# Two levels' pair products in one burst: a second place for the recurrence's factors, results in their operands' buffers, and a scheduler that knows turns of shape

## The chip, the cores and the metric

The kernel runs on one core of one Trainium2 chip. The metric is the device time of one execution in microseconds, taken as the median of several runs. TensorE (PE) multiplies matrices, and its weight loads have a row of their own (PEld); VectorE (DVE), ScalarE (ACT) and GpSimd (POOL) work on tiles of 128 partitions in on-chip memory; SyncE (SP) issues the DMA transfers. Each engine executes its own queue in order, and waits of one engine for another go over semaphores.

## The reference, cut to what matters

The input is x with 2 batches of 4096 tokens and 256 channels. Two layers of a recurrent block (time mixing, then channel mixing) are followed by a gated feed-forward part whose operands are rounded to blockwise FP4, both parts with an adaptive layer norm around them. The centre of the time mixing is this recurrence, for 4 heads of 64 channels each:

```python
def step(state, inp):
    rt, kt, vt, wt = inp
    kv = kt[..., :, None] * vt[..., None, :]
    out = jnp.einsum('bhk,bhkv->bhv', rt, state + u[None, :, :, None] * kv)
    return (state * wt[..., None] + kv, out)
```

Around it, per layer:

```python
sx = _shift(x) - x
mix = jnp.tanh((x + sx * p['x_maa']) @ p['tm_w1'])   # five small mixing products from it
wx, kx, vx, rx, gx = (x + sx * (p[n] + m) for n, m in ...)
r = sigmoid(rx @ Wr); k = kx @ Wk; v = vx @ Wv; g = silu(gx @ Wg)
w = exp(-exp(time_decay + tanh(wx @ td_w1) @ td_w2))
x = x + (norm(recurrence(r, k, v, w, time_first)) * gn_w + gn_b) * g @ Wo
x = x + sigmoid(xr @ cWr) * (square(relu(xk @ cWk)) @ cWv)   # channel mixing
...
x = x + gb * fp4_linear(silu(fp4_linear(h, w_gate)) * fp4_linear(h, w_up), w_down)
```

## The kernel before, in words

**Tiles.** A tile is 256 tokens (TT) of one batch, two chunks (C) of 128, with the 256 channels in two halves (J) of 128. There are 16 tiles per batch, so 2 layers x 2 batches x 16 tiles = 64 recurrences (`wkv`, line 799), and 32 tiles for the feed-forward part, in half tiles of 128 tokens (`ffn_chunk`, line 1304).

**The recurrence without a loop over tokens.** In a chunk of 128 tokens the product of the decays between a token s and a later token t is split by levels: at level l tokens are paired in groups of 2^l, and `r` and `k` carry the decays up to that level as factors. For each level `products(l)` (line 820) multiplies the `k` of one group with the `r` of the next on PE, with 64 rows of weights (one head) and 32 or 64 columns; a level is 32 matmuls for l = 0 to 4, 16 for l = 5, 8 for l = 6. They go into the PSUM tile `pa`. After each level DVE multiplies the totals of the decays into half of the factors, in place (`pair_view`, line 767, and the `tensor_tensor` into `upd` in line 852), and forms the totals of the next level in `tots`. Masks then pick the valid pairs out of `pa` into `diag` (DVE, `copy_predicated`, line 869), ACT copies them into `attn`, and PE multiplies `attn` with `v`, adds what the state `S` gives, and forms `kv`, the chunk's part of the next state.

Level 0 uses copies of `r` and `k` in which every second token carries the bonus `time_first` (`with_bonus`, line 772, on ACT) in two slots, so it does not need the first update's place: levels 0 and 1 are issued together after the update of l = 0. Each further level is issued by itself, since the update of l overwrites the factors that `products(l)` reads:

```python
for m in {0: (), 1: (0, 1)}.get(l, (l,)):
    products(m)
...
upd = pair_view(rk, h, n)
pl.vector.tensor_tensor(upd, upd, tv..., ALU.mult)
```

A lock (`head_lock`) lets one recurrence at a time be written down, since `pa`, `kv`, `diag` and `attn` exist once.

**The order of the work.** No engine's order is written by hand. Generators (streams) for each layer and batch, for the feed-forward inputs, its chunks, its weights and the conditioning record operations into `Plan` (line 113), which keeps a queue for each stream and gives out one operation at a time (`run`, line 320). It estimates when an operation could start, from costs (`weight`, line 386), dependencies (`need`, line 187, on bounding intervals of the operands) and free engines, and takes among the operations of an engine that could start within `SOON` of the earliest the one of the least lateness, then the oldest. Operations of PE and ACT have a form; a change of form costs `TURN` (PE 94) in its estimate, but does not decide the choice. The estimates set nothing but the order: on the chip semaphores decide.

**Buffers.** Tiles of 128x514 come from a stock of 36 slots, `r` and `k` together from 4 places of their own (`slot2`), the wide feed-forward buffers from 5 (`long`). A stream goes on only while enough slots are free (`LEAST`). Results take a new slot, and the operand's slot is given back after its last reader is written down, for example in `shifted` (line 720: `xn`, then `x`), `time_mix` (line 940: `xx` and `mix`, `xg` and `g`, `xw` and `td`, `xv` and `v`), `channel_mix` (line 1087) and `ffn_chunk` (`hb`, then `hT`).

Of the kernel before, what the change touches and what calls it, by code (L numbers as in the profile page):

```python
# [16 lines left out]
P = 128  # L17
D = 256
J = D // P
TT = 256  # L20
# [14 lines left out]
SLOTS = 36  # L35
STAGGER = (12, 60)
SLOTS2 = 4
TINY = 16
LONG = 5
# [61 lines left out]
class Op:  # L101
    __slots__ = ("eng", "calls", "cost", "port", "wait", "ready", "next", "end", "banks", "tiles", "age", "late", "forms")
# [10 lines left out]
class Plan:  # L113
# [24 lines left out]
    def __init__(self, nc, banks):  # L138
        self.nc, self.banks = nc, [(0.0, b) for b in banks]
        self.probe = banks[0]  # L140
        self.seen = {}
        self.held = {}
        self.free = {e: 0.0 for e in self.ENG}
        self.lock = {"vector": 0.0, "gpsimd": 0.0}
        self.form = {"tensor": None, "scalar": None}
        self.loaded = 0.0
        self.cur = None
        self.count = 0
        for e in self.ENG:
            setattr(self, e, Recorder(self, e))  # L150

    def comes(self, t, when):

        op = Op("load", 0)
        op.next, op.end = None, when
        self.seen[t.name] = [(op, True, 0, P, 0, 1 << 20)]
# [10 lines left out]
    def stock(self, tiles):  # L167
        for t in tiles:
            self.held[t.name] = 0
        return tiles  # L170
# [8 lines left out]
    @staticmethod  # L179
    def region(ap):  # L180
        step, n = ap.ap[0]
        p0 = ap.start_partition()
        lo = ap.offset - p0 * step if n > 1 or step else ap.offset
        hi = lo + 1 + sum((c - 1) * t for t, c in ap.ap[1:])
        return p0, p0 + n, lo, hi

    def need(self, op, ap, writes):
        if isinstance(ap, Later):
            key, probe = ap.bank, ap.probe
            if ap.bank not in op.banks:  # L190
# [7 lines left out]
        p0, p1, lo, hi = self.region(probe)  # L198
        seen = self.seen.setdefault(key, [])
        keep = []  # L200
        for q in seen:
            o, w, a, b, c, d = q
# [3 lines left out]
            if not (writes and hit and p0 <= a and b <= p1 and lo <= c and d <= hi):  # L206
                keep.append(q)
        keep.append((op, writes, p0, p1, lo, hi))
        self.seen[key] = keep
# [8 lines left out]
    def record(self, eng, fn, a, k):  # L218
        st = self.cur
        outs = [k["out"]] if "out" in k else [a[0]]  # L220
        ins = list(a[0 if "out" in k else 1:]) + [v for n, v in k.items() if n != "out"]
        ins = [v for v in ins if isinstance(v, (bass.AP, Later))]
        cost, port = weight(eng, fn, outs[0], ins)
        op = st.last if eng == "tensor" else None
        if op is None or op.next is None:
            self.count += 1
            op = Op(eng, self.count)
            op.late = st.late
            st.queue.append(op)
# [12 lines left out]
        for v in outs:  # L242
            if not is_dram(v):
                self.need(op, v, True)
# [12 lines left out]
    def turn(self, op):  # L257

        return self.TURN[op.eng] if op.forms and op.forms[0] != self.form[op.eng] else 0.0

    def give_out(self, op, t):
# [9 lines left out]
        for fn, a, k in op.calls:  # L271
            fn(*[real(v) for v in a], **{n: real(v) for n, v in k.items()})  # L272
# [35 lines left out]
    def ready(self, streams):  # L308

        can = []  # L310
        for st in streams:
            for op in st.queue:
                if op.wait:
                    continue
                t = self.start(op, st)
                if t is not None:
                    can.append((t, op.late, op.age, op, st))
        return can

    def run(self, streams, stock):  # L320
        streams = [Stream(*q) for q in streams]
        while True:
# [22 lines left out]
            if not can:  # L345
# [8 lines left out]
                (late, age, t, o, st) for t, late, age, o, st in can  # L354
# [3 lines left out]
            self.give_out(op, t)  # L358

# [26 lines left out]
def weight(eng, fn, out, ins):  # L386
# [6 lines left out]
    if eng == "tensor":  # L393
        n, rows, cols = out.free_size(), ins[0].shape[0], out.shape[0]
        if fn == "transpose":
            return 110.0, False
        if rows == P and cols == P:
            return max(4 * n / 2.4 + 6, 195.0 if n == 64 else 265.0 if n == P else 0.0), False
        if n <= 64:
            return {(64, 32): 22.0 if n > 16 else 16.0, (64, 64): 66.0, (P, 64): 70.0}.get((rows, cols), 2 * n), False  # L400
        return 0.55 * (4 * n / 2.4 + 6), False
# [14 lines left out]
    if fn in ("bn_stats", "bn_aggr", "tensor_reduce", "reciprocal"):  # L416
        two = False
    return (205.0 if fn == "scalar_tensor_tensor" and n <= 256 else 150.0) + n / 0.96, two
# [3 lines left out]
def rwkv_adaln_fp4_kernel(ctx: ExitStack, tc: tile.TileContext, a: dict, out: bass.AP):  # L422
# [297 lines left out]
    def shifted(h, ln_w, car):  # L720
# [5 lines left out]
        x_s = take_slot()  # L726
# [5 lines left out]
        give(xn_s)  # L732
# [7 lines left out]
    def lerp(x, sx, maa):  # L740
        m_s = take_slot()
# [25 lines left out]
    def pair_view(rk, h, n):  # L767

        v = rk[:, h : h + 1]
        return bass.AP(v.tensor, v.offset, [v.ap[0], [J * TT - h, 2], [2 * h, n], [1, h]])  # L770
# [28 lines left out]
    def wkv(i, b, rk_s, dec_s, v_s):  # L799
# [3 lines left out]
        r, k = (rk[:, m * J * TT : (m + 1) * J * TT].rearrange(  # L803
            "p (c j t) -> p c j t", c=C, j=J) for m in range(2))
# [4 lines left out]
        r0_s, k0_s = take_slot(), take_slot()  # L809
        r0, k0 = v4(r0_s), v4(k0_s)  # L810
# [8 lines left out]
        at = 0  # L819
        def products(l):  # L820
            R, K = (r0, k0) if l == 0 else (r, k)
# [55 lines left out]
        give(dec_s)  # L877
        tot = tot.rearrange("p (c j) -> p c j", c=C)
# [61 lines left out]
    def time_mix(i, b, h):  # L940
# [9 lines left out]
        give(xx_s)  # L950
        mix_s = take_slot()
# [5 lines left out]
        def to_input(o, maa):  # L957

            m_s = take_slot()
# [8 lines left out]
        def branch_pair(f, g, maa_f, maa_g):  # L968
# [9 lines left out]
            for bk, o, maa in zip(bks, os, (maa_f, maa_g)):  # L978
                ms.append(to_input([o[:, j * TT : (j + 1) * TT] for j in range(J)], maa))
# [14 lines left out]
        give(xg_s)  # L994
        g_s = take_slot()
# [13 lines left out]
        give(xw_s)  # L1009
        td_s = take_slot()  # L1010
# [4 lines left out]
        xk_s, xv_s = branch_pair(1, 2, w["k_maa"], w["v_maa"])  # L1015
# [27 lines left out]
        give(mix_s, x_s, sx_s)  # L1043
# [15 lines left out]
        v_s = take_slot()  # L1059
# [4 lines left out]
        give(xv_s)  # L1064
# [4 lines left out]
        give(o_s)  # L1069
        oT_s = take_slot()  # L1070
# [16 lines left out]
    def channel_mix(i, b, h):  # L1087
# [3 lines left out]
        xr, xr_s = lerp(x, sx, w["cr_maa"])  # L1091
        give(x_s, sx_s)
        yield
        kks = []
        for g in range(FD // P // 2):
# [6 lines left out]
            kks.append(take_slot())  # L1102
# [5 lines left out]
        give(xk_s)  # L1108
        sr_s = take_slot()
# [4 lines left out]
        give(xr_s)  # L1114
# [153 lines left out]
    def ffn_inputs():  # L1268
# [3 lines left out]
        for n in range(B * NT):  # L1272
# [6 lines left out]
            yield from layernorm_rows(x1, xn, rows["cb"][b], lambda c: rows["sb"][b])  # L1279
            p_s = pl.take(long)  # L1280
            yield from fp4(pl, xn_s, C * D, P, scales[0], p_s)
            long.append(p_s)
            xq_s = take_slot()
# [4 lines left out]
            give(xn_s)  # L1288
# [15 lines left out]
    def ffn_chunk(c, b, t, x1_s, xq_s, left):  # L1304
        HF = FI // 2
        cs_ = slice(c * P, (c + 1) * P)
        x1, xqT = v3(x1_s), v3(xq_s)
        hb_s = pl.take(long)
        hb = hb_s[:, :FI]
        for s in range(2):  # L1310
# [13 lines left out]
            yield  # L1324
        p_s = pl.take(long)
        yield from fp4(pl, hb_s, FI, P, scales[1 + c], p_s)
        long.append(p_s)
        hT_s = pl.take(long)
# [11 lines left out]
        long.append(hb_s)  # L1340
# [17 lines left out]


    streams = [(counted(first_layer(b), b, 0), LATE[0], LEAST[0]) for b in range(B)]  # L1360
    streams += [(counted(second_layer(b), b, 1), LATE[1], LEAST[1]) for b in range(B)]
    with tc.manual_schedule():
        for t, src, _ in coming:
            nc.sync.dma_start(out=t, in_=src)
        streams += [(ffn_inputs(), LATE[2], LEAST[2]), *((ffn_chunks(c), LATE[2], 1) for c in range(C)), (ffn_weights(), 2.0, 0), (conditioning(), -1.0, 0)]
        pl.run(streams, stock)
# [48 lines left out]
```

## Time and profile before

| what | value |
|---|---|
| time, median of 3 runs | 3134.46 us (3129.04 to 3141.4) |
| the profiled execution: time, span of its instructions | 3128.25 us, 3126.4 us |
| mean granted clock of TensorE | 0.983 |
| busy time of PE, PEld, DVE | 2995.5, 2400.8, 2386.0 us |
| busy time of ACT, POOL | 1627.4, 947.8 us |
| DMA | 42.51 MB, mean 14 GB/s |
| activation table loads on ACT | 131 of 1283 ns |

In the profile an instruction that `Plan` recorded carries the line of `give_out` (L272), so operations are told apart by their tiles: `pa<-slot` are the pair products of levels 1 to 6, `pa<-slot,slot` those of level 0, `bank<-...` all matmuls into the five rotating PSUM banks. A form 64\*32 means 64 rows and 32 columns of TensorE's array in use. A matmul in the code is two records in the trace, a transpose one. The ends of matmuls are modelled, so that distances between starts tell more than lengths.

### The profile page before, as it was taken

Reading aid. Unit: us, or ns where it says so; the run is one execution under the profiler, and the core shown is the slowest. Engines: PE = TensorE matmul, PEld = TensorE weight load, DVE = VectorE, ACT = ScalarE, POOL = GpSimd, SP = SyncE. Lnnn points to the kernel's source line nnn. Section 1 sums busy time; section 2 is a strip of 40 time slices with the busy share of each in tenths; the row PEclk is TensorE's granted clock in tenths of the full one; section 3 lists DMA queues with packets and bytes.
Section 4 is the critical chain, followed back from the end, with each engine's and each line's share of the span. In section 5 each row is a group of like instructions: output and inputs, shape, how many; then the busy total and the mean of one; then the engine's idle time right before and its main releaser. Section 6 shows DMA issues by size and latency. Waiting matters only on the chain.

```text
span 3126.4 us, 89289 instructions
## 1 busy us (share of the span) xinstructions
PE 2995.5 (96%) x38460; PEld 2400.8 (77%) x38460; DVE 2386.0 (76%) x6146; ACT 1627.4 (52%) x3366; POOL 947.8 (30%) x888
## 2 busy tenths in 40 slices
PE   6899999999999999999999999999999999999977
PEld 4777787787877777777778878778888787787765
DVE  6786777877778777778787777777877877786766
ACT  3555555555555455554555555545555555554432
POOL 2233333232332331333323333332323333332210
PEclk8899999999999999999999999999999999999988
DMA  4000000000000000000000000000000000000000
GB/s 141 23 9 5 14 9 10 9 13 9 10 8 10 13 8 7 16 7 15 5 8 15 7 15 8 14 5 14 7 9 15 8 12 7 9 7 12 10 7 12
DMA packets 35723, 42.51 MB, mean 14 GB/s; under 512 B 2817, under 2 KB 33537, under 8 KB 35329
## 3 DMA queue, kind: packets, MB, share of 16 engines
q1 hardware_dynamic: 35328, 36.81, 3.8%
q8 instruction: 302, 4.95, 0.7%
q14 instruction: 93, 0.75, 0.1%
HBM read 28.41 MB, written 8.39 MB: 12 GB/s over the span
## 4 chain that ended last, share of the span: by engine, by line
PE 81%; DVE 10%; ACT 6%; issue 2%; POOL 1%; DMA 0%; POOLq 0%; DVEq 0%; ACTq 0%; SPq 0%
PE bank L272 72%; PE pa L272 7%; DVE slot L272 5%; ACT slot L272 3%; DVE long L272 2%; ACT attn L272 2%; PE kv L272 1%; DVE tiny L272 1%; DVE scales L272 1%; POOL slot L272 1%; DVE diag L272 1%; ACT L272 0%; POOL tiny L272 0%; ACT long L272 0%; DVE S L272 0%
## 5 line engine op out<-in xcount | busy, mean ns | idle before, releaser
L272 POOL TENSOR_TENSOR slot<-slot,slot 128x512 f32<-128x512 f32 (+1 forms) x448 | 514.6, 1162 | 898.2 <-DVE slot L272 666.2
L272 ACT ACTIVATE slot<-bank 128x512 f32<-128x512 f32 (+2 forms) x644 | 333.0, 521 | 690.2 <-PE bank L272 662.7
L272 POOL TENSOR_TENSOR tiny<-tiny,nhalf 128x2 f32<-128x2 f32 (+1 forms) x288 | 291.5, 1015 | 962.7 <-DVE tiny L272 893.9
L272 DVE TENSOR_TENSOR slot<-slot,slot 128x512 f32<-128x512 f32 x512 | 386.8, 757 | 104.4 <-PE pa L272 86.3
L272 PE MATMUL bank<-slot,small 32*128 32x256 f32 (+3 forms) x2816 | 401.9, 362 | 3.6 <-DVE slot L272 3.1
L272 PE MATMUL bank<-slot,cWk 128*128 128x256 f32 x1536 | 373.1, 389 | 6.9 <-DVE slot L272 6.4
L272 PE MATMUL bank<-cWv,slot 128*128 128x256 f32 x1536 | 343.9, 380 | 0.0
L272 PEld LDWEIGHTS bank<-slot,small 32*128 32x128 f32 (+3 forms) x2816 | 269.6, 178 | 90.6 <-issue 38.9
L272 PEld LDWEIGHTS pa<-slot 64*32 64x32 f32 x19456 | 221.8, 107 | 139.1 <-issue 51.5
L272 PEld LDWEIGHTS bank<-slot,cWk 128*128 128x128 f32 x1536 | 285.5, 193 | 51.4 <-DVE slot L272 7.9
L272 PEld LDWEIGHTS bank<-cWv,slot 128*128 128x128 f32 x1536 | 289.2, 190 | 40.3 <-ACT slot L272 0.3
L272 ACT ACTIVATE slot<-bank,small 128x256 f32<-128x256 f32 (+1 forms) x640 | 251.9, 451 | 79.9 <-PE bank L272 78.1
L272 DVE SCALAR_TENSOR_TENSOR slot<-bank,small,slot 128x256 f32<-128x256 f32 x640 | 274.9, 474 | 23.7 <-PE bank L272 22.7
L272 PE MATMUL pa<-slot 64*32 64x16 f32 x19456 | 263.7, 190 | 30.2 <-DVE slot L272 16.6
L272 DVE TENSOR_TENSOR slot<-slot,bank 128x512 f32<-128x512 f32 x192 | 131.0, 683 | 180.9 <-PE bank L272 159.9
L272 POOL TENSOR_TENSOR slot<-slot 128x512 f32<-128x512 f32 x128 | 141.5, 1106 | 311.6 <-ACT slot L272 217.1
L272 ACT ACTIVATE slot<-slot 128x512 f32<-128x512 f32 x288 | 182.0, 635 | 34.3 <-DVE slot L272 30.0
L272 ACT ACTIVATE slot<-slot,tiny 128x256 f32<-128x256 f32 x256 | 142.0, 594 | 106.3 <-DVE tiny L272 85.5
L272 DVE TENSOR_TENSOR long<-long,bank 128x352 f32<-128x352 f32 x256 | 131.7, 516 | 85.9 <-ACT long L272 64.8
L272 DVE SCALAR_TENSOR_TENSOR slot<-slot,small,slot 128x256 f32<-128x256 f32 x384 | 181.0, 507 | 17.5 <-POOL slot L272 17.4
L272 PE MATMUL bank<-ident,slot 128*128 128x128 f32 x1152 | 177.8, 282 | 12.9 <-ACT slot L272 7.7
L272 PE MATMUL bank<-wd,long 128*128 128x256 f32 x768 | 187.3, 395 | 2.0 <-ACT long L272 1.4
(106 smaller groups left out, 5347.9 us busy)
## 6 DMA issues: line engine op xcount, KB each, us to landing
slot<-in_L_attn_x_dram SPq DMA_DIRECT2D x64, 256.0 KB, 2.8
out_dram<-slot SPq DMA_DIRECT2D x64, 128.0 KB, 1.7
slot<-in_L_wmod_dram SPq DMA_DIRECT2D x6, 256.0 KB, 7.6
cWk<-in_L_attn_cWk_dram SPq DMA_DIRECT2D x2, 768.0 KB, 7.9
cWv<-in_L_attn_cWv_dram SPq DMA_DIRECT2D x2, 768.0 KB, 9.9
small<-in_small_dram SPq DMA_DIRECT2D x2, 718.0 KB, 8.5
long<-in_L_ffn_w_down_dram SPq DMA_DIRECT2D x2, 352.0 KB, 3.1
long<-in_L_ffn_w_gate_dram SPq DMA_DIRECT2D x5, 128.0 KB, 8.1
```

Of the source, the lines that this page charges most:

```text
L272: fn(*[real(v) for v in a], **{n: real(v) for n, v in k.items()})
```

## The change

It has three parts.

1. **A second place for the factors.** One tile `rk2` of 128x1024 takes the factors of levels 0, 3 and 4; the others stay in the `slot2` place (`place`). The update from level 2 to 3 reads one place and writes the other, and so does that from 4 to 5; the half that the update does not multiply is copied by ACT. Products of levels 0 and 1, 2 and 3, and 4 and 5 are recorded together, level 6 by itself. The copies of level 0 go into `rk2` in place of two slots.
2. **Results in their operands' buffers.** `x` takes the slot of `xn`, `mix` of `xx`, `g` of `xg`, `td` of `xw`, `v` of `xv`, `oT` of `o`, the last mixed input that of `sx`, and in the feed-forward part `xq` that of `xn` and `hT` that of `hb`. Slots go from 36 to 37, places for `r` and `k` from 4 to 3, `long` from 5 to 4. Streams wait for a free place or `long` buffer before they take one.
3. **The scheduler.** An operation of PE that changes the form is put behind others by `TURNS`, and a turn back to 128\*128 costs `BACK` more. Regions of operands are exact bit sets in place of bounding intervals (`spread`). Some costs are set anew. The order of equal lateness gets a random part (`JITTER`), eight orders are drawn up without writing them down (`dry`), and the one whose estimated end is earliest is written.

The core of the diff:

```diff
-SLOTS = 36
+BACK = 104.0
+TURNS = 30.0
+SLOTS = 37
 STAGGER = (12, 60)
-SLOTS2 = 4
+PLANS, JITTER = 8, 8.0
+SLOTS2 = 3
 TINY = 16
-LONG = 5
+LONG = 4
...
-        hi = lo + 1 + sum((c - 1) * t for t, c in ap.ap[1:])
-        return p0, p0 + n, lo, hi
+        dims = tuple((t, c) for t, c in ap.ap[1:] if t and c > 1)
+        return p0, p0 + n, spread(dims) << lo
...
-            hit = a < p1 and p0 < b and c < hi and lo < d
+            hit = a < p1 and p0 < b and c & at
...
+            op.rank = op.age + self.random.uniform(0.0, JITTER)
...
-        return self.TURN[op.eng] if op.forms and op.forms[0] != self.form[op.eng] else 0.0
+        if not op.forms or op.forms[0] == self.form[op.eng]:
+            return 0.0
+        return self.TURN[op.eng] + (BACK if op.forms[0] == (P, P) else 0.0)
...
-                (late, age, t, o, st) for t, late, age, o, st in can
+                (late, age + TURNS * (o.eng == "tensor" and self.turn(o) > 0), t, o, st) for t, late, age, o, st in can
                 if o.eng == op.eng and t <= now + SOON
...
+    rk2 = keep.tile([P, 2 * J * TT], F32, name="rk2")
...
+    def parts(rk):
+
+        return (
+            rk[:, m * J * TT : (m + 1) * J * TT].rearrange("p (c j t) -> p c j t", c=C, j=J) for m in range(2)
+        )
+
+    def pair_view(rk, h, n, changed=True):
+
+        v = rk[:, h : h + 1] if changed else rk[:, :1]
+        return bass.AP(
+            v.tensor, v.offset, [v.ap[0], [J * TT - h if changed else J * TT + h, 2], [2 * h, n], [1, h]]
+        )
...
-        r0_s, k0_s = take_slot(), take_slot()
-        r0, k0 = v4(r0_s), v4(k0_s)
+        r0, k0 = parts(rk2)
+        r, k = parts(rk)
...
+        place = {0: rk2, 1: rk, 2: rk, 3: rk2, 4: rk2, 5: rk, 6: rk, 7: rk}
+
         def products(l):
-            R, K = (r0, k0) if l == 0 else (r, k)
+            R, K = parts(place[l])
...
-            for m in {0: (), 1: (0, 1)}.get(l, (l,)):
+            for m in {1: (0, 1), 3: (2, 3), 5: (4, 5), 6: (6,)}.get(l, ()):
                 products(m)
-            if l == 1:
-                give(r0_s, k0_s)
...
-            upd = pair_view(rk, h, n)
+            here, there = place[l] if l else rk, place[l + 1]
+            if here is not there:
+                pl.scalar.copy(pair_view(there, h, n, False), pair_view(here, h, n, False))
             pl.vector.tensor_tensor(
-                upd, upd, tv.rearrange("p n m -> p m n").unsqueeze(3).to_broadcast([P, 2, n, h]), ALU.mult
+                pair_view(there, h, n), pair_view(here, h, n), tv.rearrange("p n m -> p m n").unsqueeze(3).to_broadcast([P, 2, n, h]), ALU.mult
             )
...
-        x_s = take_slot()
+        x_s = xn_s
...
-        v_s = take_slot()
+        v_s = xv_s
...
-        hT_s = pl.take(long)
+        hT_s = hb_s
...
+    def plan(seed, dry):
+
+        pl.begin(seed, dry)
...
+        return max(pl.free.values())
+
+    best = min(range(PLANS), key=lambda seed: plan(seed, True))
```

More of the change, by code (lines that the diff above doesn't have):

```diff
@@ L101 @@
 class Op:
-    __slots__ = ("eng", "calls", "cost", "port", "wait", "ready", "next", "end", "banks", "tiles", "age", "late", "forms")
+    __slots__ = ("eng", "calls", "cost", "port", "wait", "ready", "next", "end", "banks", "tiles", "age", "late", "forms", "rank")
     def __init__(self, eng, age):
@@ L358, in run, with spread @@
             self.give_out(op, t)
+@lru_cache(None)
+def spread(dims):
+    m = 1
+    for t, c in reversed(dims):
+        k, out = 1, m
+        while k < c:
+            s = min(k, c - k)
+            out |= out << t * s
+            k += s
+        m = out
+    return m
 class Stream:
@@ L1307, in ffn_chunk @@
         x1, xqT = v3(x1_s), v3(xq_s)
+        while not long:
+            yield
         hb_s = pl.take(long)
@@ L1324, in ffn_chunk @@
             yield
+        while not long:
+            yield
         p_s = pl.take(long)
@@ L1364, in rwkv_adaln_fp4_kernel @@
             nc.sync.dma_start(out=t, in_=src)
-        streams += [(ffn_inputs(), LATE[2], LEAST[2]), *((ffn_chunks(c), LATE[2], 1) for c in range(C)), (ffn_weights(), 2.0, 0), (conditioning(), -1.0, 0)]
-        pl.run(streams, stock)
+        plan(best, False)
 def layout(inputs):
```

116 lines of the change are left out of this document (67 added, 49 removed).

## The prediction

> **What bounds the kernel now.** I read the page's engine row and slices first, then the windows by stage, then PE's timeline.
>
> ```profile
> span 3126.4 us, 89289 instructions
> PE 2995.5 (96%) x38460; PEld 2400.8 (77%) x38460; DVE 2386.0 (76%) x6146; ACT 1627.4 (52%) x3366; POOL 947.8 (30%) x888
> ...
> PE   6899999999999999999999999999999999999977
> ...
> PE 81%; DVE 10%; ACT 6%; issue 2%; POOL 1%; DMA 0%; POOLq 0%; DVEq 0%; ACTq 0%; SPq 0%
> PE bank L272 72%; PE pa L272 7%; DVE slot L272 5%; ACT slot L272 3%; DVE long L272 2%; ACT attn L272 2%; PE kv L272 1%; DVE tiny L272 1%; DVE scales L272 1%; POOL slot L272 1%; DVE diag L272 1%; ACT L272 0%; POOL tiny L272 0%; ACT long L272 0%; DVE S L272 0%
> ```
>
> PE is full in all slices but the first two and the last two, and 81% of the chain that ended last is PE. The windows by stage (time, then busy time and count of PE, weight loads, DVE, ACT, POOL, then PE's granted clock) say how full:
>
> ```profile
> 100.00:200.00 100.00, 91.93 (x1041) 75.21 (x1041) 82.26 (x226) 55.28 (x120) 36.35 (x31) 0.95 0.06 16
> 200.00:2900.00 2700.00, 2651.23 (x34921) 2135.49 (x34920) 2075.49 (x5364) 1459.74 (x3014) 852.22 (x780) 1.00 0.04 10
> 2900.00:3127.00 227.00, 182.49 (x1510) 141.48 (x1508) 158.79 (x351) 77.26 (x153) 35.89 (x35) 0.90 0.03 10
> ```
>
> Between 200 and 2900 us PE lacks 49 us of 2700 and runs at the full clock. So a microsecond taken from PE's own stream is a microsecond of the end, as long as nobody is late for PE. But a busy PE is not a working PE: the ends of matmuls are modelled, so dead time between two shapes of matmul hides in it. The timeline shows it (start, length to the last end, operation, count of records; each matmul in the code is two records):
>
> ```profile
> 1502.35 0.73 PE L272 MATMUL pa<-slot 64*32 64x16 f32 x64
> 1503.01 1.99 PE L272 MATMUL bank<-slot,small 128*128 128x256 f32 x8
> 1504.94 0.45 PE L272 MATMUL pa<-slot 64*32 64x32 f32 x32
> 1505.32 0.66 PE L272 MATMUL bank<-ident,slot 128*128 128x128 f32 x4
> ```
>
> Read starts alone. A record 128x256 in a run of its like takes 0.216 us (16 of cWk from 1530.60 to 1534.06). Eight take 1.73, but from 1503.01 to 1504.94 it is 1.93: the turn from the full shape 128\*128 to 64\*32 costs 0.20. A product record takes 0.0083 (64 of them in 0.53 us when another product level follows, 1491.59 to 1492.12). 64 take 0.53, but 1502.35 to 1503.01 is 0.66: turning back costs 0.13. Over all 268 and 251 such turns of the timeline the medians are **0.198 and 0.129 us**, with the middle half within 0.001; 0.182 is that of leaving 32\*128. A visit of PE to the pair products costs 0.327 us beside its work.
>
> **The change, part by part.**
>
> *Turns of shape.* The instruction order of the two programs can be counted, since the scheduler writes it out. Matmuls are 20016 in both. Runs of one shape: 128\*128 from 597 to 431, 64\*32 from 313 to 189, 32\*128 from 164 to 142, the others from 253 to 241. Separate visits to the tile pa fall from 373 to 252, because levels 0 and 1, 2 and 3, 4 and 5 now stand in one visit. With the price of leaving each shape: 166 x 0.198 = 32.9, 124 x 0.129 = 16.0, 22 x 0.182 = 4.0, the others 1.1: **54.0 us** less. The joined levels alone are 124 x 0.327 = 40.5 of it; the other 13.5 is the scheduler's new dislike of turns (BACK, TURNS), mostly in the small mixing matmuls. All of it lies on PE, which sets the end.
>
> The Trainium skill, TensorEngine Tiling (Array Packing), Key Properties, says that changing the tiling mode drains the array; it gives no price there. TensorE: Matmul & The Clock Gate, Step-by-step, puts the drain at some 128 cycles, which at 2.4 GHz is 0.053 us: an estimate by that page is 0.107 for both turns, and the 54 would be some 18. The row has three times that, and is what I use.
>
> *The waits at the products.* I laid the durations above over PE's order, which gives the PE work from each level's products to the next level's. Against the starts in the trace the median difference is 0.02 us or less for each step, so what is left are waits: 7.4, 12.3, 12.7, 5.2 and 8.0 us over 64 recurrences for the five steps from level 1 to 6, 45.6 together. Steps 2 to 3 and 4 to 5 go (17.5 us). Two of the three steps left now need two updates in a row on DVE, and there the cover counts. Median PE work between the visits is 2.92 us (levels 1 to 2), 2.76 (3 to 4) and 2.06 (5 to 6); before it was 2.05 at most steps.
>
> *The copies.* Levels 3 and 5 need their factors in another place than levels 2 and 4, so the half that is not multiplied is copied by ACT: 2 x 64 = 128 copies of 128x512. The page's rows for the parts:
>
> ```profile
> L272 DVE TENSOR_TENSOR slot<-slot,slot 128x512 f32<-128x512 f32 x512 | 386.8, 757 | 104.4 <-PE pa L272 86.3
> ...
> L272 ACT ACTIVATE slot<-slot 128x512 f32<-128x512 f32 x288 | 182.0, 635 | 34.3 <-DVE slot L272 30.0
> ```
>
> 128 x 0.635 = 81 us on ACT, 52% to 55%: hidden there. What is not hidden: at l=2 the waits written into the program make the update into rk2 wait for the copy into rk2 in 46 of 64 recurrences, and the copy wait for the update in most of the rest; though they touch different halves, they run one after the other. (At l=4 both wait for the same update and run beside each other.) So from the last product of level 1 to the first of level 2 it takes update 0.757, copy 0.635, update 0.757 and four handovers of about 0.1 to 0.15: 2.7 us against the cover of 2.92; 29 of 64 have less than 2.7, and their shortfalls add up to 22 us. Behind the waiting update on DVE stand the next tile's statistics and mixing, for which PE waits too; between the two updates only 0.42 us of other DVE work remains. Ends: 0, if PE's other work covers it, and 64 x 0.83 (copy and two handovers) = 53, if all of it reaches PE. I take 20, near the sum of shortfalls. With the 17.5 saved, waits come out even within 5.
>
> *Buffers.* Results written over operands (x over xn, g over xg, v over xv, hT over hb and so on) add no instruction; each result already had to wait for the readers of that operand. Slots 36 to 37 with fewer taken, long 5 to 4 with hT inside hb, rk places 4 to 3: I cost these at 0. The work of the other streams hides a late buffer; without it, a stream that waits for a third rk place stalls by up to one recurrence. One rk2 for all: the next bonus must wait for the previous level 4; in the trace it starts earlier than that in 9 of 63 cases, by 5.0 us at most, and the bonus stands a median of 12.8 us ahead of its first product. So 0; the other end is 9 x 5 = 45 us of PE idle, far off since four streams feed PE.
>
> *The scheduler.* Exact regions in place of bounding ones, corrected costs, eight orders tried: no cost on the chip. The gain lies between 0 and the 49 us that PE lacks from 200 to 2900. I take 0, since the two other rows of waits are already counted.
>
> *The end.* From 2980 on DVE's fp4 chains set the pace (PE idle 11.5 us before one transpose of long). After the last kv product 9 half tiles of the FFN follow before, 7 after, with 98 and 84 us of PE work, so the tail shrinks with the rest and the 54 is not lost there.
>
> Sum against the profiled execution: it took 3128.25 (span 3126.4 and 1.9 around it). 3128 - 54 - 17 + 20 = 3077. The median shown, 3134.5, lies 6 above that execution; I put the forecast half-way up, at **3080 us**.
>
> **The rivals.**
>
> *The waits eat the gain* (chance 0.15). For it: 57 of 64 gaps between the two updates hold under 0.85 us of DVE work, so DVE stops there. All of the 53 us reach PE and only the 17.5 come back: 3128 - 54 - 17 + 53 = 3110, or 3128 if the gain of the joined steps fails too. Against it: four streams, and waits at the same places cost 0.08 to 0.20 us a step now.
>
> *Slower* (0.05). One mechanism: the stretch from level 1 to level 2. The updates take 1.76 (at 1492.95) and 1.10 (at 1496.39) when POOL works beside them, and an activation table load of 1.283 (131 in the trace) can stand ahead of the copy on ACT. If that were the rule, the stretch needs 1.10 + 1.28 + 0.64 + 1.10 + 0.5 = 4.6 against 2.92: 1.7 x 64 = 109, and 3128 - 54 + 109 = 3183. It decides from a mean of 0.84 us per recurrence (54 / 64). Against it: the mean of the update is 0.757, and there are two table loads per recurrence in some 49 us.
>
> *PE is not the bound* (in the first rival's 0.15). Weight loads are busy 77% of the span and DVE 76%; if PE's turns were slack that waits elsewhere would fill, the time would stay at 3128. Against it: the 49 us of PE idle in 2700, and turns of the same length in every place, which a wait would not have. By the Trainium skill, Perfetto Trace Analysis, Identifying the Most-Contended Engine, matmul busy time is no measure of the distance to the peak and weight loads are the better one, which speaks for this rival.
>
> *More than forecast* (0.20). Half of the 49 us goes as well: 3128 - 54 - 25 = 3049, 3055 as a median.
>
> The change not doing what it says is excluded for the order: the joined visits stand in it, 122 of 64 matmuls and 3 of 128.
>
> **How the numbers follow.** Forecast 0.60 at 3080, its own range 3065 to 3098. The range that should hold 8 in 10 takes in the better case and the first rival's lower part: 3048 to 3118. Half a per cent, about what a measurement can tell here, is 16 us: 3119. Faster: 0.60 + 0.20 + 0.07 of the first rival = 0.87; same 0.08; slower 0.05.
>
> **What would show it.** In the profile after: about 125 fewer rows of pa in the timeline and turns still at 0.198 and 0.129; PE busy near 2940; ACT with 128 copies near 0.64 us; DVE idle before the rk2 update released by ACT. Wrong it would be if PE's idle from 200 to the tail rose from 49 to over 80, or if the update's mean rose above 0.8.

## The result, and the profile after

| what | before | after |
|---|---|---|
| time, median of 20 runs each | 3133.3 us (3129.0 to 3141.4) | 3142.2 us (3131.6 to 3152.1) |
| ratio to before, 95% interval | | 1.0023 [1.0015, 1.0031] |
| span of the profiled execution, mean granted clock | 3126.4 us, 0.983 | 3135.3 us, 0.976 |

The changed kernel is 9 us slower, within the half per cent that counts as no change, where 3080 had been forecast; the range ended at 3118. The traces come from single executions, of 3128.3 us before and 3137.2 after, both about 5 below their medians. The page of the changed kernel, its first rows and slices:

```profile
span 3135.3 us, 89669 instructions
...
PE 2965.8 (95%) x38460; PEld 2417.5 (77%) x38460; DVE 2359.7 (75%) x6146; ACT 1684.7 (54%) x3492; POOL 946.2 (30%) x888
...
PE   6899999999999999999999999999999999998997
```

PE is busy 30 us less and the span is 9 us longer. Its windows (time, then busy time and count of PE, weight loads, DVE, ACT, POOL, then PE's granted clock):

```profile
100.00:200.00 100.00, 90.99 (x952) 75.06 (x952) 72.91 (x213) 52.88 (x111) 32.55 (x31) 0.87 0.05 15
200.00:2900.00 2700.00, 2604.10 (x34592) 2135.37 (x34590) 2040.11 (x5320) 1498.05 (x3103) 838.57 (x767) 0.98 0.03 10
2900.00:3136.00 236.00, 205.34 (x1934) 161.40 (x1934) 179.00 (x416) 97.11 (x196) 51.30 (x49) 0.97 0.04 12
```

Between 200 and 2900 us PE now lacks 96 us, not 49, and gets through 34592 records, not 34921. The clock column fell from 1.00 to 0.98: in the record of the granted clock the time at 0.5 in this stretch rose from 17 to 85 us. PE's waits there (who waits, for whom; us, times, longest), before, then after:

```profile
PE pa L272 <- DVE slot L272: 8.7, 14, 1.5
...
PE pa L272 <- DVE diag L272: 3.7, 3, 2.2
```

```profile
PE pa L294 <- DVE diag L294: 19.3, 21, 2.6
PE bank L294 <- ACT slot L294: 15.4, 20, 2.3
PE pa L294 <- DVE slot L294: 10.2, 10, 3.3
```

The largest is new: products wait until a predicated copy into `diag` is done. One such place in the timeline of the changed kernel (start, length, engine, operation, count, and in brackets the idle time before it with its releaser):

```profile
1599.32 0.71 PE L294 MATMUL pa<-slot 64*32 64x16 f32 x62
...
1599.96 1.56 PE L294 MATMUL bank<-slot,small 32*128 32x256 f32 x12
...
1600.92 0.68 DVE L294 TENSOR_TENSOR slot<-slot,slot 128x512 f32<-128x512 f32 x1
...
1601.52 0.43 DVE L294 COPY_PREDICATED diag<-masks,pa 128x256 f32<-128x256 int32 x1
1601.69 0.62 ACT L294 COPY rk<-slot 128x512 f32<-128x512 f32 x1 [4.82 <-DVE slot L294]
...
1602.34 0.69 DVE L294 TENSOR_TENSOR rk<-slot,slot 128x512 f32<-128x512 f32 x1 [0.39 <-ACT rk L294]
1602.95 0.43 DVE L294 COPY_PREDICATED diag<-masks,pa 128x128 f32<-128x128 int32 x1
...
1603.44 0.76 PE L294 MATMUL pa<-slot 64*32 64x16 f32 x60 [1.92 <-DVE diag L294]
```

Levels 0 and 1 end at 1600.03. Level 1's update runs at 1600.92, then ACT's copy, and level 2's update only when the copy is done (1601.69 + 0.62 = 1602.31; it starts at 1602.34): three steps in a row. The predicated copies of levels 0 and 1 stand on DVE between them, and the products of level 2 wait for the second one, to 1603.38. PE had one piece of other work, and then 1.92 us of nothing. What follows the wait shows in four windows around it:

```profile
1596.60:1600.00 3.40, 3.40 (x142) 2.83 (x140) 2.61 (x7) 0.27 (x1) 1.57 (x1) 1.00 0.00 0
1600.00:1603.40 3.40, 1.52 (x14) 1.04 (x12) 2.70 (x6) 1.69 (x2) 0.97 (x2) 1.00 0.13 43
1603.50:1606.90 3.40, 3.40 (x132) 2.61 (x133) 3.31 (x10) 0.11 (x1) 2.27 (x2) 0.50 0.02 5
1606.90:1610.30 3.40, 3.40 (x46) 2.38 (x45) 2.53 (x5) 1.57 (x3) 1.73 (x2) 1.00 0.00 0
```

PE worked 1.52 of 3.40 us, and in the next 3.4 us its clock is 0.50. PE's rows there:

```profile
1604.05 0.81 PE L294 MATMUL pa<-rk 64*32 64x16 f32 x62
1604.79 2.48 PE L294 MATMUL bank<-wg,slot 128*128 128x352 f32 x4
1607.11 1.89 PE L294 MATMUL bank<-slot,Wg 128*128 128x256 f32 x8
1608.84 1.35 PE L294 MATMUL bank<-wu,slot 128*128 128x352 f32 x4
1610.11 0.73 PE L294 MATMUL pa<-rk 64*32 64x16 f32 x64
```

By the starts, the four records of 128x352 from 1604.79 take 2.32 us, and the four from 1608.84, at the full clock, 1.27. The products are hardly slower: the 128 records from 1603.44 take 1.35 us, where the medians before (2 x 0.53 and a turn back) give 1.2. So the wait cost 1.9 us, and the clock after it some 1.2 more.

**Where the 9 us come from.** As in the prediction I price PE's instructions and turns at their medians before, in program order, and subtract this from the measured distance between the first products of two levels; the rest is waits and lost clock ("excess"), summed over 64 recurrences. The priced order falls from 2939 to 2886 us, so 53 are saved. Excess of the six steps between levels, 0 to 1 first, goes from 5.5, 7.4, 12.3, 12.7, 5.2, 8.0 to 3.9, **46.3**, 1.0, **34.3**, 1.8, **20.8**: 57 us more. From level 6 over kv to the next recurrence it is 25 more, at the start 4 more, behind the last kv 24 less. -53 + 57 + 25 + 4 - 24 = +9.

### The profile page after: what moved, and what is told of

Same layout as the page of the kernel before. It is cut to its first block, busy times and chain, and to the rows that moved or that the text cites. A ratio compares the mean times of both kernels' runs of the same rounds, so it can differ in the third digit from the quotient of the medians.

```text
span 3135.3 us, 89669 instructions
## 1 busy us (share of the span) xinstructions
PE 2965.8 (95%) x38460; PEld 2417.5 (77%) x38460; DVE 2359.7 (75%) x6146; ACT 1684.7 (54%) x3492; POOL 946.2 (30%) x888
## 5 line engine op out<-in xcount | busy, mean ns | idle before, releaser
L294 PE MATMUL bank<-slot,small 32*128 32x256 f32 (+3 forms) x2816 | 391.8, 363 | 13.0 <-DVE slot L294 7.1
L294 DVE TENSOR_TENSOR slot<-slot,slot 128x512 f32<-128x512 f32 x320 | 235.5, 738 | 69.9 <-PE pa L294 37.3
L294 PE MATMUL pa<-slot 64*32 64x16 f32 x11264 | 173.9, 195 | 37.2 <-DVE slot L294 15.8
L294 PEld LDWEIGHTS pa<-slot 64*32 64x32 f32 x11264 | 145.5, 111 | 79.6 <-DVE diag L294 23.7
```

## The experiments

Theory 1: the joined levels themselves make the waits (two updates and a copy in a row, four predicated copies ahead of level 4). Theory 2: the scheduler's edits make them. Theory 3: the buffers. Theory 4: the order drawn is a matter of luck. An edit of the scheduler or of the work changes the whole order, so each run but e3, whose order is that of the changed kernel, has a plan of its own. In the table "priced" is the sum over PE's order as above, "idle" is PE's from 200 to 2900 us, "at 2" is the part of it that lies just ahead of level 2's products, and "half" is the time at granted clock 0.5 in the same stretch; all in us. The last four columns come from one execution each, which lies up to 10 us from the run's median (e12_unpaired 10 below it, e1_place and e13_pa_only 8 above), and "half" differs between executions of one kernel: small differences in these columns tell nothing.

| run | time | ratio to before, 95% | priced | idle | at 2 | half |
|---|---|---|---|---|---|---|
| before | 3133 to 3138 | 1 | 2939 | 49 | 7.1 | 17 |
| after | 3142.2 | 1.0023 [1.0015, 1.0031] | 2886 | 96 | 18.4 | 85 |
| e1_place | 3120.0 | 0.9950 [0.9934, 0.9965] | 2905 | 67 | 1.6 | 96 |
| e2_sched | 3162.5 | 1.0089 [1.0065, 1.0112] | 2926 | 94 | 20.5 | 62 |
| e3_cols | 3143.1 | 1.0023 [1.0009, 1.0037] | 2886 | 97 | 18.2 | 82 |
| e4_nocopy | 3099.6 | 0.9890 [0.9868, 0.9912] | 2882 | 78 | 5.6 | 67 |
| e5_bounds | 3115.0 | 0.9938 [0.9922, 0.9955] | 2884 | 67 | 0.4 | 55 |
| e6_buffers | 3155.3 | 1.0064 [1.0042, 1.0087] | 2906 | 77 | 0.4 | 65 |
| e7_no_turns | 3177.5 | 1.0144 [1.0126, 1.0161] | 2898 | 109 | 26.0 | 86 |
| e8_seed3 | 3155.5 | 1.0075 [1.0060, 1.0090] | 2888 | 95 | 26.0 | 85 |
| e9_more_bufs | 3105.8 | 0.9912 [0.9896, 0.9928] | 2887 | 67 | 0.6 | 55 |
| e10_long4 | 3102.5 | 0.9900 [0.9876, 0.9925] | 2882 | 70 | 0.6 | 48 |
| e11_bufs_alone | 3151.8 | 1.0074 [1.0048, 1.0099] | 2906 | 84 | 0.0 | 68 |
| e12_unpaired | 3138.5 | 1.0012 [0.9999, 1.0026] | 2921 | 64 | 8.8 | 38 |
| e13_pa_only | 3139.8 | 1.0010 [0.9998, 1.0022] | 2880 | 93 | 2.5 | 85 |
| e14_rk_only | 3100.5 | 0.9886 [0.9869, 0.9902] | 2888 | 69 | 3.1 | 51 |
| e15_sched_bounds | 3153.8 | 1.0054 [1.0034, 1.0073] | 2923 | 72 | 7.5 | 58 |
| e16_old_costs | 3135.9 | 0.9989 [0.9977, 1.0000] | 2898 | 77 | 1.8 | 72 |
| e17_one_edge | 3124.9 | 0.9969 [0.9955, 0.9982] | 2882 | 72 | 4.7 | 72 |
| e18_rk_more_bufs | 3071.4 | 0.9794 [0.9780, 0.9809] | 2890 | 57 | 4.1 | 31 |

### One part alone, and the suspects on their own

**e1_place.** Before, with `rk2`, `place`, the joined bursts and the copies, and `-SLOTS = 36` / `+SLOTS = 34`.

> The kernel before with only the second place and the joined levels (old scheduler, old buffers otherwise, 34 slots so that it fits). Theory 1 (the joined levels themselves lengthen the chain between two visits to pa: two updates in a row, the copy ahead of the one at level 2, four predicated copies ahead of level 4; TensorE waits there and its clock is halved afterwards): TensorE's idle from 200 to 2900 us 80 to 110 us and half-clock time there 60 to 100 us as in the changed kernel, time 3120 to 3160. Theory 2 (the scheduler's edits make the waits): idle 40 to 60, half-clock about 20, time 3070 to 3095, which is the time before less the 40 us of turns of shape.

17 us faster than the kernel before beside it (3136.5). Of the 34 us saved in priced order about half arrives. The step 1 to 2 has 23 us of excess, not 46, and PE hardly stands ahead of level 2 (1.6). The half-clock time of 96 us belongs to the slowest of its ten executions (3127.8 us, mean clock 0.972); the median of the mean clock is 0.978 here, 0.979 in the kernel before beside it and 0.974 in the changed kernel, so a usual execution loses hardly more clock than the kernel before. So the joined levels do cost waits, as theory 1 has it, but they gain on the whole.

**e2_sched.** Before, with the third part of the change alone.

> The kernel before with only the scheduler's edits (exact regions, price of a turn, jitter and eight plans, corrected costs), levels and buffers as before. Theory 1: idle and half-clock time as before (about 50 and 20 us from 200 to 2900), time 3105 to 3135, the lower end if fewer turns of shape are made. Theory 2: idle 80 or more, half-clock 60 or more, time over 3150. The scheduler's own estimate of the end is 50 us above that for the kernel before, so by its own reckoning this one is slower: if the chip follows, about 3180.

26 us slower, though its order is priced 13 lower: theory 2 holds for a large part. That -17 and +26 make +9, the whole change, can be chance: results in their operands' buffers are in neither, and each number holds to within the size of a draw of the plan (see e8). Its waits look like those of the changed kernel, without the new joins (levels 2 with 3 and 4 with 5) and without a copy:

```profile
PE pa L294 <- DVE diag L294: 23.9, 28, 2.3
PE bank L294 <- ACT slot L294: 14.1, 22, 2.5
```

**e3_cols.** After, so that levels 0 to 5 share no column of `pa`.

```diff
-        at = sum(wide[0 if l < 4 else 4 : l])
+        at = sum(wide[0 if l < 6 else 6 : l])
```

> The changed kernel, with columns of pa of their own for levels 0 to 5, so that level 4's products no longer wait until the four predicated copies of levels 0 to 3 have read pa. Theory 1: the step from level 3 to level 4 loses about 1.4 us less on VectorE per recurrence, its excess of 34 us falls to about 15, some half-clock time goes with it: 3105 to 3125. If the two updates and not the predicated copies bind there: excess stays near 30, time 3135 to 3145.

No change (excess of 3 to 4: 37, `PE pa <- DVE diag` 23.3 over the whole span against 24.2). My reason was wrong: products and predicated copies that share no element are put in order all the same, so columns of their own do not part them.

**e4_nocopy.** After, without

```diff
-            if here is not there:
-                pl.scalar.copy(pair_view(there, h, n, False), pair_view(here, h, n, False))
```

> The changed kernel with both ScalarE copies between the two places left out, so the half of the factors that an update doesn't change is stale after levels 2 and 4 (the output isn't the reference's). Theory 1: from the end of level 1 to the update of level 2 1.2 us less, the excess of the step 1 to 2 falls from 46 to about 15 us: time 3080 to 3110. Rival (the copies are covered, the two updates bind alone): excess over 35, time 3130 to 3145. Rival (order of the plan): the plan drawn is another one, so a change of more than 25 us at unchanged excess per step would be the order's.

This version leaves half of the factors stale after levels 2 and 4, so it is a measurement and no alternative. 43 us faster than the changed kernel; excess of 1 to 2 is 16. The copies, 2 x 64 of 0.618 us on an engine that is busy 54%, matter, it seems, through the order that they force, since the engine that runs them has idle time left.

### Which of the scheduler's edits

**e5_bounds.** After, with the intervals of the kernel before:

```diff
-        dims = tuple((t, c) for t, c in ap.ap[1:] if t and c > 1)
-        return p0, p0 + n, spread(dims) << lo
+        n1 = 1 + sum((c - 1) * t for t, c in ap.ap[1:])
+        return p0, p0 + n, ((1 << n1) - 1) << lo
```

> The changed kernel, but its scheduler takes the region of an access as the whole interval from its first to its last element again, so it plans the copy and the update at level 2 one after the other, as the chip runs them. Theory 2a (exact regions make the scheduler blind to an order that the program has all the same): the excess of the step 1 to 2 falls from 46 to about 20 us as in the run with the second place alone, half-clock time falls with it: 3110 to 3125. Theory 1 (the joined levels alone): 3135 to 3150.

27 us faster than the changed kernel, excess of 1 to 2 is 20, and PE's waits of pa for `diag` are down to

```profile
PE pa L294 <- DVE diag L294: 3.9, 7, 1.1
```

**e6_buffers.** e5 with `-TURNS = 30.0` / `+TURNS = 0.0` and `JITTER` 0.001.

> The changed kernel with interval regions, no price of a turn and no jitter (one plan): what is left of the change is the second place, the buffers that results take over, and the corrected costs. Next to the run with the second place alone (3120): if the buffers cost nothing, 3110 to 3130. If single slots and fewer buffers bind (theory 3), 3140 or more.

**e7_no_turns.** After, with `-TURNS = 30.0` / `+TURNS = 0.0`.

> The changed kernel with the price of a turn out of the choice of the next instruction (exact regions, jitter and seed as before). It makes some 11 us more of turns by my count. If holding the products back to save a turn is what makes the waits, their sum falls by more than 25 us: 3115 to 3130. If exact regions make them, the excess of the step 1 to 2 stays at 35 or more and the time is 3140 to 3160.

**e8_seed3.** After, with `-    best = min(range(PLANS), ...)` / `+    best = 3`.

> The changed kernel with the plan of another draw (seed 3; its estimated end is 10.4 us above that of the plan taken). If the scheduler's estimate tells plans apart, 3145 to 3160; if draws differ on the chip by their waits and not by the estimate, anything within 30 us of 3142, and this is the size below which two plans tell nothing of a cause (theory 4).

The price of a turn is worth 35 us with exact regions (e7 against after) and, with the draw of plans, 40 with intervals (e6 against e5), though it saves only 12 and 22 us of priced order; it is not what makes the waits. Another draw is 13 us slower: differences of that size between two plans prove no cause. It is a single pair, so the spread of draws may well be wider; and the kernel before, measured beside each group of runs, moved from 3133 to 3138, which adds some 4 us of doubt between groups. In e7 and e8 PE idles 26 us ahead of level 2, in e5 and e6 0.4: that number goes with the regions, whatever the draw.

### Buffers and joining, with interval regions

**e9_more_bufs** is e5 with 34 slots, 4 places, 5 long buffers; **e10_long4** with 35, 4, 4; **e11_bufs_alone** is e6 with the numbers of e9.

> The changed kernel with interval regions (3115 with the buffers of the change) and the second place's bytes taken from 3 of the 37 slots instead: 34 slots, 4 places of the recurrence's factors, 5 long buffers. Best of eight plans by the scheduler's estimate (seed 2). If the fewer buffers bind (theory 3), the waits from the products of level 6 to the next recurrence's level 0 (36 and 56 us of excess) shrink by some 20 us: 3085 to 3105. If not, within 15 us of 3115.

> As the one before with 35 slots, 4 places of the factors and 4 long buffers as in the change (seed 1, the scheduler's estimate 4 us lower). If the places of the factors bind, as the one before; if the long buffers do, 10 us or more over it.

> The run with interval regions, no price of a turn and no jitter (3155), with 34 slots, 4 places of the factors and 5 long buffers. The one difference is the numbers of buffers. Theory 3: back to 3120 to 3130, as with the second place alone. If results that take their operands' buffers, or the corrected costs, lose the time: 3145 or more.

9 and 13 us faster than e5, but e11 only 3 faster than e6 (by the ratios to the kernel before, 3 slower): all within the size of a draw. Theory 3 is not confirmed; these runs can't tell whether the numbers of buffers are worth anything. e6 and e11 stay 32 to 35 us above e1, which the next group takes up.

**e12_unpaired.** e5 with levels 2 to 5 a burst each:

```diff
-        place = {0: rk2, 1: rk, 2: rk, 3: rk2, 4: rk2, 5: rk, 6: rk, 7: rk}
+        place = {0: rk2, 1: rk, 2: rk, 3: rk, 4: rk, 5: rk, 6: rk, 7: rk}
...
-            for m in {1: (0, 1), 3: (2, 3), 5: (4, 5), 6: (6,)}.get(l, ()):
+            for m in {0: (), 1: (0, 1)}.get(l, (l,)):
```

> The changed kernel with interval regions (3115), but levels 2 to 5 each a burst of their own as in the kernel before, and no copy between the places (the second place holds level 0's factors alone). If joining is worth its turns less the waits that I saw (34 less some 17): 3130 to 3145. If joining cost more than it saved (theory 1 in full): under 3110.

23 us slower than e5. Joining is worth about that: 37 us of priced order, less what its waits cost. It is more than a draw, and e1 points the same way without the new scheduler, so theory 1 in full, that joining costs more than it saves, has fallen.

### Which order the exact regions lose

In the built programs one can read what each instruction waits for. In the changed kernel the first products of level 2 wait for a predicated copy in 52 of 64 recurrences; under intervals (e5) always for level 1's update. At l=2 the update waits for the copy in 47 and the copy for the update in 17; e5 has the copy first in all 64, since its plan knows that the two do not run together. The traces agree: 47 and 64 copies start ahead of their update, and in neither kernel do the two overlap once.

**e13_pa_only**, **e14_rk_only.** After, with intervals for one kind of tile:

```diff
+        if ap.name.startswith("pa"):                # e14: (("rk2", "slot2"))
+            n1 = 1 + sum((c - 1) * t for t, c in ap.ap[1:])
+            return p0, p0 + n, ((1 << n1) - 1) << lo
```

> The changed kernel with interval regions for pa alone (exact ones elsewhere, the best of eight plans by the scheduler's estimate, seed 3). In the built program of the changed kernel the first products of level 2 wait for the predicated copy of level 1 in 52 of 64 recurrences, because the planner, with exact regions, puts the predicated copies of levels 0 and 1 ahead of them; here they wait for level 1's update in all. If that order is the larger part of the 27 us of exact regions: excess of the step 1 to 2 about 30 us, 3115 to 3128. If the copy that the planner takes to run beside its update is: 40 us or more, 3132 to 3145.

> The other half: interval regions for the two places of the factors alone (seed 5), so the planner knows that level 2's update waits for the copy, and the predicated copies still go ahead of level 2's products (56 of 64 recurrences). If the copy's wait is the larger part: 3115 to 3128; if the predicated copies are: 3132 to 3145.

With `pa` alone nothing is gained (3139.8): the predicated copies stand behind the products again and the idle time ahead of level 2 is 2.5, but the step 3 to 4 has 46 us of excess and idle and half-clock time are as long as before the edit. With the factors alone 42 us are gained, more than with intervals everywhere (27), though the difference is the size of a draw. DVE's update into `rk2` in the changed kernel, then in e14 (count, busy us, mean ns, idle before it and its releaser), and e14's wait for `diag`:

```profile
L294 DVE TENSOR_TENSOR rk<-slot,slot 128x512 f32<-128x512 f32 x64 | 44.2, 691 | 16.6 <-ACT rk L294 16.6
```

```profile
L297 DVE TENSOR_TENSOR rk<-slot,slot 128x512 f32<-128x512 f32 x64 | 44.9, 702 | 3.3 <-ACT rk L297 3.3
```

```profile
PE pa L297 <- DVE diag L297: 4.8, 8, 1.1
```

The update hardly waits for the copy any more, since the plan puts other work between them; the predicated copies still go ahead of level 2's products in e14, and PE hardly waits for them. So in the changed kernel it is an order among the factors that hurts, most likely the copy's, and the wait for `diag` was the last link of a chain that had become late through it. That the copy alone does it is not shown: e14 gives the plan all orders of the factors, and e2, which has no copy, waits as long for `diag` (23.9 us).

**e15_sched_bounds**: e2 with e5's diff. **e16_old_costs**: e11 with the costs and the price of a turn of before.

> The kernel before with the scheduler's edits but interval regions (the run with exact ones took 3162; the scheduler's estimates of the two differ by 0.3 us). No joined levels and no copies here. If exact regions let predicated copies go ahead of products also in this kernel: excess of the steps 1 to 2 and 2 to 3 from 32 and 23 back to some 10 each, time 3120 to 3140. If not: 3155 or more.

> The run with 34 slots, no price of a turn, no jitter and interval regions (3152), with the instruction costs and the price of a turn that the scheduler of the kernel before had. What it has of the change beyond the second place (3120) is then only that results take their operands' buffers. If the corrected costs lost the 32 us: 3110 to 3130. If the shared buffers did: 3145 or more.

e15 is 9 us faster than e2, and its excess of the steps 1 to 2 and 2 to 3 is 16 and 18 (32 and 23 in e2). The waits at these steps go with exact regions here too, but 9 us of time is less than a draw, and 17 us of the scheduler's loss stay. e16 is 16 us faster than e11, and by the ratios to the kernel before beside each, 1.0074 and 0.9989, it is 27. So the corrected costs may take half of those 32 us or more; the rest, between e16 and e1, may be shared buffers or the draw. Neither is more than hinted at by one plan each.

**e17_one_edge.** After, and the plan is told one thing:

```diff
+                copied = pl.cur.queue[-1]            # after pl.scalar.copy(...)
...
+            if l == 2:
+                pl.edge(copied, pl.cur.queue[-1])    # after the update
```

> The changed kernel with one edge added to the planner's graph: level 2's update comes after level 2's copy (exact regions stay, everywhere; best of eight plans by the estimate, seed 1). If this one order that the program keeps and the plan did not know is what the interval regions of the factors gave back (3100): 3100 to 3115, excess of the step 1 to 2 from 46 to about 25 us. If it was another order among the factors: 3125 to 3145.

17 us faster than the changed kernel, 10 short of what I expected; excess of 1 to 2 is 39.5, not 25. PE's idle time fell from 96 to 72, that ahead of level 2 from 18.4 to 4.7, and DVE's update waits 1.6 us for the copy, not 16.6. The one edge takes the waits at its place away. It does not give all of e14's gain, and part of the waiting only moves: within the step 1 to 2, over the whole span, PE's idle time ahead of level 2 falls from 25 to 5 us, but that ahead of the other work between the two levels rises from 12 to 18, and PE's busy time at half clock there from 15 to 33.

**e18_rk_more_bufs.** e14's diff with 34 slots, 4 places, 5 long buffers (seed 2).

> Interval regions for the two places of the factors alone (3100) with 34 slots, 4 places of the factors and 5 long buffers (seed 2; the estimate is 4 us lower). If the gains of the two add up as they did with interval regions throughout (9 us): 3088 to 3098. If the plan's draw is most of that: within 12 us of 3100 on either side.

The best version, 2.1% faster than the kernel before (1.9 to 2.2) and 17 us better than I expected. Its page:

```profile
span 3069.1 us, 89705 instructions
...
PE 2940.4 (96%) x38460; PEld 2397.5 (78%) x38460; DVE 2374.5 (77%) x6146; ACT 1688.0 (55%) x3494; POOL 954.0 (31%) x888
...
PE   6889999999999999999999999999999999999997
```

Idle 57 us, half-clock 31. That is about the state that the forecast had assumed: the priced saving of 49 us arrives whole and some more with it, at 3071 against 3080. How much of the 29 us from e14 is buffers and how much the draw stays open.

The scheduler's own estimate sees next to nothing of this: its ends for the plans of after, e13, e14 and e18 are 3002, 3003, 3001 and 2996 us, and the chip took 3142, 3140, 3100 and 3071.

## Why the prediction was wrong, by its own steps

- **Turns of shape, -54: right.** The priced order fell by 53 us, and the prices held: medians of 0.198 us into 64\*32, and back 0.129 behind one level and 0.145 behind two, before as after.
- **Waits of the steps 2 to 3 and 4 to 5, -17.5: right.** 12.3 to 1.0 and 5.2 to 1.8, together -14.7.
- **The copies, +20 (ends 0 and 53): mis-sized.** The serial copy was seen, but the step 1 to 2 rose by 39 us. Two terms were missing: the predicated copies that the new plan puts between the updates, and the clock that is halved after a wait. The steps 3 to 4 (+22) and 5 to 6 (+13) I had taken as covered. Even without the scheduler's edits the joined levels gain 17 us (e1), not the 34 of their priced order, so the waits do not come out even there either.
- **"The scheduler: no cost on the chip. I take 0", with a gain as the only other end: this is the step that failed.** The edits of the scheduler alone cost 26 us (e2), of which exact regions explain some 9 (e15); the rest may be the corrected costs (e16), but that isn't shown. In the changed kernel exact regions cost 27 (e5), and this is where the reading failed. I had read in the program that update and copy at l=2 run one after the other, and not asked whether the new planner knows it. With exact regions it does not, and it places PE's products for a chain that is one copy (0.62 us) shorter than the real one; giving it the orders of the factors was worth 42 us (e14), the one edge alone 17 (e17), little more than a draw.
- **Buffers 0: within what the runs can tell**; their number moved the time by 3 to 13 us where regions were intervals throughout. Results over operands are what e16 has beyond e1: 16 us slower, about a draw.
- **The tail 0:** 24 us of excess behind the last kv went; a gain that I had not counted.
- **"Wrong it would be if PE's idle rose from 49 to over 80": it rose to 96.** The first rival (the waits eat the gain, 3110 to 3128) names what happened; its price left out the clock. The time at half clock grew by 68 us (85 - 17). If all work ran at half speed in it, 34 us would be lost; but products hardly slow down, and over the 128 executions of the changed kernel and the 18 experiments, each compared within its kernel, a microsecond of lost clock (1 - mean clock, times the time) goes with 0.7 us of time, which makes about 24 an estimate. With the idle time's 47 that is some 70 of the 82 us of excess added in the steps and around kv (57 + 25). The other sign, an update above 0.8 us, did not come: 0.69 into `rk2`.

What stays open: the idle time ahead of matmuls other than products, kv and attn rose from 19 to 42 us and is 31 to 53 in all runs but the one before. It wasn't taken apart. That e14 gains more than e17 (by 24 us) and e5 (by 15) is measured; which orders among the factors, or how much luck of the draw, make the difference is not.

## What to carry to other kernels

A planner that orders instructions by its own dependency graph must know every wait that the built program will hold, the needless ones too: a sharper graph than the program's made the plan look as good and run worse. When an edit touches the planner, list the waits of the built program beside the edges of its graph, and price the edit by the one part alone. Where TensorE is the bound, a wait of a microsecond or two can cost more than its length: here 47 us of waits drew some 24 of slower matmuls after them. And before an edit of a planner is called better or worse, draw several orders: two draws differed by 13 us here, as much as several of the single edits.

## What the runs showed of the hardware

The granted clock drops to 0.5 after waits much shorter than I had thought. In the kernels before and after there are 23 such drops between 200 and 2900 us, of 3.4 or 6.8 us each; in the 3.4 us ahead of one PE was idle for a median of 1.6 us (0.65 to 3.2 in 22 of the 23), in all other stretches at full clock for 0.06 on average. There is no sharp threshold in these numbers: some stretches with up to 1.7 us of idle time kept the full clock, and one drop came after 0.35. At 0.5 a record 128x256 in a run of its like takes 0.427 us against 0.216, while product records stay near 0.01 us each.

The Trainium skill, TensorE: Matmul & The Clock Gate, HAM oscillation — how this bites in real kernels, gives the rule that idle gaps should stay under some 3.4 us; by it the wait of 1.92 us at 1601.5 would have been free of this. The record shows 0.50 right behind it, so the measurement decides: half a stretch of idle time can be enough here.
